# Cross-attention block: in half of the attention's units, scores are computed a second time with the keys on partitions instead of being turned, and the values' bias is added to the attention's result

## The chip, the cores and the metric

The kernel runs on one core of a Trainium2 chip. The metric is the time of one execution on the device, in microseconds (us), as the median of several runs. One execution was also recorded by the hardware profiler; where the text speaks of the profile or of the trace, it is that one.

## What is computed

The reference is one transformer block with cross-attention, in float32. Of B = 8 batches here, each has 256 tokens `x` and 256 context tokens, of width 512, with 16 heads of 32 elements.

```python
x = layer_norm(hidden_states, ln1_w, ln1_b)
q = (x @ q_w + q_b)   # split into 16 heads of 32
k = (encoder_hidden_states @ k_w + k_b)
v = (encoder_hidden_states @ v_w + v_b)
scores = einsum('bhqd,bhkd->bhqk', q, k) * scale
scores = where(mask, scores, mask_value)
out = einsum('bhqk,bhkd->bhqd', softmax(scores, axis=-1), v)
hidden = out @ cproj_w + cproj_b + hidden_states
y = layer_norm(hidden, ln2_w, ln2_b)
y = gelu(y @ fc_w + fc_b, approximate=True)      # 512 -> 2048
return hidden + y @ proj_w + proj_b              # 2048 -> 512
```

## The kernel before

**Groups and stages.** The eight batches are worked in two groups `g` of four. For each group there are stages, called streams: `ctx` (load and turn the context), `x` (load, normalise and turn the tokens), `k`, `q`, `v` (projections), `core` (attention), `o` (output projection), `y` (second normalisation), `fc` and `pr` (the two layers of the MLP). `fw` and `pw` make sums of the MLP's weights and store them in DRAM once, for both groups to load. The matrix products are made by a fast scheme of seven block products instead of eight (`quad`), in the MLP twice nested (`grown`, `grown2`); its sums of blocks are what `sums`, `plus` and `minus` issue on VectorE (DVE) or GpSimd (POOL), with names such as `z1i` or `y0t`. The products of one `quad` go to PSUM banks X, Y and W, from which `take` (a copy, on ScalarE (ACT) or DVE) or `plus` (an addition, on DVE) moves each result to SBUF.

**Attention.** A unit is four heads `hg` of one batch `b`; a group has 16 units. `scores` loads `q`, `k` and `v` of the unit, makes the group of matmuls `s` (eight matmuls on 32 rows of the array each, four heads side by side, into four banks, queries on partitions), adds the mask and takes each row's maximum on DVE (line 841, eight operations), and exponentiates on ACT with the row's sum accumulated (line 847, eight operations). The inverse sums and the maxima are turned on DVE (line 854), stored in DRAM (`rd`) and the inverse sums loaded back as `R` with queries along the free axis. `attend`, two units later (`LOOK = 2`), brings keys onto partitions: 16 turns on TensorE (PE) by the identity (line 870, tile `ps_pt`), four copies to `pt` (`take`), then the group `av` (eight matmuls, 32 columns of the array each), and the multiplication by `R` into the tile `att`.

**Bias of the values.** In `values_of` every fresh result of a `quad` is added to `vb`, the bias broadcast over all partitions, on the way out of PSUM. Other biases that lie along partitions come as columns: the vectors are loaded as rows, turned by PE (line 576) and kept in `cols`.

**Order.** Nothing is placed by hand. Every operation is entered into an `Order` with the engines that may run it and an estimated cost on each (`dve(n)`, `act(n)`, `pool(n)`, and given numbers), and with the tiles that it reads and writes. `times` gives each operation a due time: operations on PE from the window of their stage in `WINDOWS`, the others from their users, with `LEADS` for loads. `run` then goes through a planned execution and picks, for each engine that is free, the ready operation that is due first, within limits (`AHEAD`, `BORROW`, and `SWITCH` for a change of the array's shape, and free tiles and banks). Banks are three of a kind W and five of a kind C, of which C may be lent to W. Where an operation has several engines, this decides which gets it; operations marked `lock` are not planned on DVE and POOL at once. The instructions are issued in that order, so each engine works through a fixed list and waits where an input is late. All loads and stores are issued by one queue, SyncE (SP).

Of the kernel before, what the change touches and what calls it, by code (L numbers as in the profile page):

```python
# [12 lines left out]
U8 = mybir.dt.uint8  # L13
# [4 lines left out]
P = 128  # L18
# [11 lines left out]
BORROW = 25.6  # L30
SWITCH = 0.0

AHEAD = {"PE": 1000.0, "DVE": 66.7, "ACT": 36.8, "POOL": 25.4, "SP": 26.9}
# [19 lines left out]
class Order:  # L53
# [83 lines left out]
    def run(self):  # L137
# [29 lines left out]
        for o in ops:  # L167
            o.waiting = len(o.deps)
            o.ready = 0.0
        def offer(o):  # L170
            for e, _ in o.alts:
                cands[e].append(o)
        for o in ops:
            if not o.waiting:
                offer(o)
# [42 lines left out]
        while left:  # L218
            best = None
            for e in engines:  # L220
                pick, when = None, None
                soonest = None
                free = max(at[e], lanes[n_dma % DMA_LANES]) if e == "SP" else at[e]
                for o in cands[e]:
                    t = max(free, o.ready)
                    if soonest is None or t < soonest:
                        soonest = t
                if soonest is None:
                    continue
                t = max(soonest, skip[e])  # L230
# [6 lines left out]
            for o in cands[e]:  # L237
                if max(at[e], o.ready) > t + 1e-9:
                    x = max(at[e], o.ready)
                    again = x if again is None else min(again, x)  # L240
                    continue
# [87 lines left out]
            for x, _ in o.alts:  # L329
                cands[x].remove(o)  # L330
# [39 lines left out]
def pool(n):  # L370
# [11 lines left out]
    "ctx0": (2.1, 3.1, 6.2),  # L382
    "e0": (6.3, 7.3, 8.3),
    "e1": (2.7, 9.7, 23.1),
    "k0": (2.2, 19.8, 66.5),
    "x0": (41.0, 42.0, 52.6),
    "q0": (36.1, 69.2, 76.3),
    "v0": (51.8, 77.6, 120.0),
    "core0": (68.9, 154.0, 221.0),
    "ctx1": (81.1, 83.7, 113.7),  # L390
    "k1": (110.4, 118.8, 159.6),
    "v1": (152.1, 164.2, 181.7),
    "x1": (165.9, 169.4, 170.4),
    "q1": (191.8, 204.0, 224.7),
    "fw0": (42.7, 70.6, 89.3),
    "fw1": (104.3, 111.0, 140.7),
    "pw0": (140.8, 166.0, 168.9),
    "pw1": (181.8, 200.1, 227.1),
    "core1": (211.4, 327.0, 411.1),
    "o0": (225.3, 240.2, 271.2),  # L400
    "y0": (278.0, 297.0, 300.0),
    "fc0": (276.1, 365.9, 419.5),
    "o1": (427.1, 428.1, 463.4),
    "y1": (433.2, 448.9, 450.7),
    "pr0": (422.3, 480.5, 534.1),
    "fc1": (488.4, 556.6, 620.7),
# [849 lines left out]
```

## Time and profile before

| what | value |
|---|---|
| time, median of 3 runs | 720.68 us (718.65 to 720.99) |
| profiled execution, time | 720.62 us |
| profiled execution, span from first to last instruction | 718.6 us |
| granted TensorE clock, mean | 0.997 |
| PE busy, matmuls | 699.8 us, 4753 instructions |
| PE busy, weight loads (PEld) | 563.0 us |
| DVE busy | 592.1 us, 1382 instructions |
| ACT busy | 294.5 us, 829 instructions |
| POOL busy | 281.3 us, 261 instructions |
| DMA, share of 16 engines' time | 62.7%, 143.19 MB |

Busy time is the time in which an engine had at least one instruction under way. A float32 matmul appears as two instructions on PE. Matmuls overlap: the duration of one is longer than the distance to the next. On DVE and ACT, too, the next instruction starts some 0.1 us before the last one has ended, so the text uses distances from start to start where work is added up. Lines of the trace name a tile or tensor by what the program called it, without numbers; a tile's memory is reused, so a name in the trace may be that of an earlier tenant.

### The profile page before, as it was taken

The page shows a single profiled execution, that of the slowest core. Times are in us where ns is not written, and L with a number is a line of the kernel's source. Part 1 is how long each engine was busy: PE and PEld are TensorE (multiplying, and loading weights), DVE is VectorE, ACT ScalarE, POOL GpSimd, SP SyncE. Part 2 cuts the span into 40 slices and gives each one's busy share as a digit, 9 for nine tenths or more (in the row PEclk, how much of TensorE's full clock was granted, in tenths as well). Part 3 has the DMA queues.
Part 4 walks back from the last instruction along what each step waited for, and adds up shares of the span by engine and source line. Part 5 has one row for each costly group of instructions (what it writes and reads, how often), then busy time and mean ns, then how long its engine had stood idle before and what let it go on. Part 6 is the DMA issues. An engine that isn't in the chain of part 4 may idle for free.

```text
span 718.6 us, 13665 instructions
## 1 busy us (share of the span) xinstructions
PE 699.8 (97%) x4753; PEld 563.0 (78%) x4753; DVE 592.1 (82%) x1382; ACT 294.5 (41%) x829; POOL 281.3 (39%) x261
## 2 busy tenths in 40 slices
PE   6999999998999999999999999999999999998997
PEld 5555675566755687877788799999989988897997
DVE  2889589987898889888988867996579898997992
ACT  2243278657576656745659840120000107610000
POOL 1383046581563700030104588364677004843000
PEclk9999999999999999999999999999999999999999
DMA  7968875998789855274534743468666557730741
GB/s 232 327 205 313 306 252 183 283 337 283 206 281 317 278 183 169 78 219 146 161 94 143 256 123 100 148 204 245 183 180 182 160 157 246 278 103 1 247 150 59
DMA packets 119332, 144.06 MB, mean 200 GB/s; under 512 B 14136, under 2 KB 82272, under 8 KB 119264
## 3 DMA queue, kind: packets, MB, share of 16 engines
q1 hardware_dynamic: 119264, 143.19, 62.7%
q8 instruction: 38, 0.62, 0.4%
q14 instruction: 30, 0.25, 0.1%
HBM read 98.59 MB, written 44.56 MB: 199 GB/s over the span
## 4 chain that ended last, share of the span: by engine, by line
PE 90%; DVE 6%; DMA 2%; issue 1%; SPq 0%; POOL 0%; DVEq 0%; POOLq 0%
PE fc_X L541 13%; PE pr_X L541 13%; PE ps_pt L870 7%; PE fc_W L541 7%; PE pr_W L541 7%; PE s L541 5%; PE av L541 4%; PE k_X L541 4%; PE o_X L541 4%; PE q_X L541 4%; PE v_X L541 3%; PE fc_Y L541 3%; PE pr_Y L541 3%; PE o_W L541 2%; PE q_W L541 2%; PE v_W L541 2%
## 5 line engine op out<-in xcount | busy, mean ns | idle before, releaser
L847 ACT ACTIVATE pr<-pr,st 128x256 f32<-128x256 f32 x256 | 127.4, 502 | 82.3 <-DVE st L841 80.8
L841 DVE CUSTOM_DVE_ANT_0 pr<-s,mb 128x256 f32<-128x256 f32 x256 | 92.4, 418 | 10.1 <-PE s L541 9.9
L1030 ACT ACTIVATE h<-h,cols 128x256 f32<-128x256 f32 x128 | 54.3, 499 | 55.7 <-DVE h L532 52.7
L870 PEld LDWEIGHTS ps_pt<-ident,pr 128*128 128x128 f32 x512 | 59.4, 141 | 18.5 <-issue 5.6
L870 PE MATMUL ps_pt<-ident,pr 128*128 128x128 f32 x512 | 70.1, 275 | 2.4 <-DVE st L841 1.9
L532 DVE TENSOR_TENSOR h<-fc_X,h 128x512 f32<-128x512 f32 x80 | 54.3, 685 | 8.3 <-PE fc_X L541 8.1
L512 ACT COPY pt<-ps_pt 128x512 f32<-128x512 f32 x88 | 49.1, 579 | 24.6 <-PE ps_pt L870 20.5
L847 ACT ACTIVATION_READ_ACCUMULATOR pr<-pr,st 128x1 f32 x256 | 48.9, 191 | 0.0
L532 DVE TENSOR_TENSOR h<-fc_W,h 128x512 f32<-128x512 f32 x48 | 32.9, 686 | 5.3 <-PE fc_W L541 3.7
L541 PE MATMUL s<-ku,qu 32*128 32x256 f32 x512 | 36.9, 400 | 0.0
L541 PE MATMUL av<-pt,vu 128*32 128x256 f32 x512 | 35.0, 385 | 0.0
L541 PEld LDWEIGHTS s<-ku,qu 32*128 32x128 f32 x512 | 23.4, 184 | 13.5 <-issue 12.0
L512 ACT COPY e<-pr_X 128x256 f32<-128x256 f32 x4 | 1.5, 373 | 76.7 <-PE pr_X L541 76.7
L532 POOL TENSOR_TENSOR h<-h,fl 128x512 f32<-128x512 f32 x8 | 11.1, 1396 | 55.5 <-DVE fl L532 54.9
L541 PEld LDWEIGHTS av<-pt,vu 128*32 128x32 f32 x512 | 14.3, 109 | 20.1 <-issue 6.6
L532 DVE TENSOR_TENSOR po<-pr_X,po 128x256 f32<-128x256 f32 x40 | 16.7, 417 | 14.3 <-PE pr_X L541 14.3
L512 DVE COPY pt<-ps_pt 128x512 f32<-128x512 f32 x40 | 26.8, 683 | 1.8 <-PE ps_pt L870 1.1
L841 DVE DVE_READ_ACCUMULATOR2_ANT st<- 128x1 f32 x256 | 21.0, 82 | 0.0
L649 POOL TENSOR_TENSOR rs_y<-rs_y,neg_half 128x2 f32<-128x2 f32 x8 | 6.7, 836 | 35.8 <-DVE rs_y L646 35.7
L530 POOL TENSOR_TENSOR z0t<-h,h 128x512 f32<-128x512 f32 x12 | 15.0, 1272 | 13.3 <-PE fc_X L541 11.6
L530 POOL TENSOR_TENSOR z0i<-z0t,z0t 128x512 f32<-128x512 f32 x10 | 16.4, 1660 | 6.3 <-DVE y1t L532 3.3
L532 DVE TENSOR_TENSOR att<-av,r 128x256 f32<-128x256 f32 x32 | 13.4, 418 | 6.5 <-PE av L541 3.9
(643 smaller groups left out, 1841.7 us busy)
## 6 DMA issues: line engine op xcount, KB each, us to landing
fl<-prd SPq DMA_DIRECT2D x21, 256.0 KB
fl<-fcd SPq DMA_DIRECT2D x19, 256.0 KB
fw<-in_L_xattn_fc_w_dram SPq DMA_DIRECT2D x16, 256.0 KB
ku<-kd SPq DMA_DIRECT2D x32, 128.0 KB
vu<-vd SPq DMA_DIRECT2D x32, 128.0 KB
qu<-qd SPq DMA_DIRECT2D x32, 128.0 KB
r<-rd SPq DMA_DIRECT2D x32, 128.0 KB
pw<-in_L_xattn_proj_w_dram SPq DMA_DIRECT2D x32, 128.0 KB
```

The lines of the kernel that those rows point to most:

```text
L512: (nc.scalar.copy if e == "ACT" else nc.vector.tensor_copy)(to(), of_())
L530: nc.gpsimd.tensor_tensor(to()[:, ts(k, 512)], in0()[:, ts(k, 512)], in1()[:, ts(k, 512)], op)
L532: E[e].tensor_tensor(to(), in0(), in1(), op)
L541: nc.tensor.matmul(o(), l(), r(), start=first, stop=True, skip_group_check=True)
L649: lambda e, rs=rs: nc.gpsimd.tensor_tensor(tile_of(rs)[:, 2:4], tile_of(rs)[:, 0:2], neg_half[:, 0:2], ALU.pow), lock=True)
L841: nc.vector.tensor_tensor_reduce(at(p_, pk), at(sb[j], i), tile_of(mb), scale=-SCALE, scalar=FLT_MAX, op0=ALU.add, op1=ALU.min, accum_out= ...
L847: nc.scalar.activation(at(p_, pk), at(p_, pk), AF.Exp, bias=tile_of(st)[:, 8 + c : 9 + c], scale=-1.0, accum_out=tile_of(st)[:, 16 + c : 1 ...
L870: nc.tensor.transpose(at(ps, 2 * kc + i, 1, P), at(pr[j // 2], 2 * (j % 2) + i)[:, ts(kc, P)], ident.t)
L1030: lambda e, f=f, b=b, c=c: nc.scalar.activation(at(h[f][b], c), at(h[f][b], c), AF.Gelu_apprx_tanh, bias=col(c_fcb + f * 4 + c), scale=1.0 ...
```

## The change

In the units of `TWICE` (16 of the 32, eight in each group) the 16 turns and four copies are left out. Instead the maxima, which `rd` holds beside the inverse sums, are loaded as a second tile `M`, broadcast over all partitions (512 KB each). `attend` makes the scores again with `k` and `q` exchanged (group `t`, eight matmuls on 32 rows, into four banks, keys on partitions), subtracts the maxima on DVE (`sub`, four operations of 512 elements) and exponentiates in place on ACT (four operations of 512 elements), with the mask as a column for each half of the keys (`mcols`, made from rows of the mask that are turned with the other vectors). The first pass of scores, with its sums, stays as it is. The other 16 units turn as before.

The values' bias is no longer added in `values_of`; `vb` is a column, and a new operation adds it to `att` after the multiplication by `R`, on POOL, ACT or DVE. Further edits: the first half of group 0's context is turned tile by tile into four banks (`fine`); six `quad`s of `fc0` (`APART`) and the two of `o0` copy their fresh results out of PSUM and add in a second operation; the planner's constants `BORROW`, `SWITCH`, `AHEAD`, `WINDOWS` and `LEADS` have other values (the windows are not shown), and its bookkeeping of candidates is written anew.

```diff
-BORROW = 25.6
-SWITCH = 0.0
-AHEAD = {"PE": 1000.0, "DVE": 66.7, "ACT": 36.8, "POOL": 25.4, "SP": 26.9}
+BORROW = 30.3
+SWITCH = 0.82
+AHEAD = {"PE": 1000.0, "DVE": 70.9, "ACT": 33.0, "POOL": 25.4, "SP": 23.5}
...
+TWICE = {(g, hg, b) for g in range(2) for hg in range(4) for b in range(4) if (hg // 2 + b // 2) % 2 == 0}
+APART = {(f"fc{g}", p, s) for g in range(1) for p in (6, 5, 3) for s in range(2)}
...
-    vecs = [(ln1_w, 4), (ln1_b, 4), (q_b, 4), (k_b, 4), (ln2_w, 4), (ln2_b, 4), (fc_b, NF)]
+    vecs = [(ln1_w, 4), (ln1_b, 4), (q_b, 4), (k_b, 4), (ln2_w, 4), (ln2_b, 4), (fc_b, NF), (v_b, 4)]
     n_rows = sum(n for _, n in vecs)
-    rows = fixed("rows", [n_rows, P], keys=len(vecs))
+    n_cols = 64 + 2 * B
+    rows = fixed("rows", [n_cols, P], keys=len(vecs) + 1)
+    mrows = fixed("mrows", [n_cols, P], U8)
     cols = fixed("cols", [P, n_rows])
+    mcols = fixed("mcols", [P, 2 * B])
+    nc.gpsimd.memset(rows.t, 0.0)
...
+        load("mrows", mrows, None, lambda: mrows.t[64:, :], lambda: mask.rearrange("b (k p) -> (b k) p", p=P), 0.01)
+        T.op("mrows", [("DVE", 0.22)], [(mrows, None)], [(rows, [len(vecs)])],
+             lambda e: nc.vector.tensor_scalar_add(rows.t[64:, :], mrows.t[64:, :], -1.0))
...
+        T.op("mcols", [("DVE", 0.12)], [(ps, None)], [(mcols, None)],
+             lambda e: nc.vector.tensor_scalar(mcols.t, tile_of(ps)[:, 64:n_cols], FLT_MAX, SCALE, ALU.mult, ALU.mult))
+        for b, v in ((cb, cproj_b), (pb, proj_b)):
...
-    def turned(g, tag, tiles, copy):
+    def turned(g, tag, tiles, copy, fine=False):
         R = [[Buf(f"{tag}{g}_{J}{L}", "Q", 4) for L in range(2)] for J in range(2)]
         for L in range(2):
+            if fine and L == 0:
+                ps = [Buf(f"ps_{tag}{g}_{a}{L}", "C", 4) for a in range(4)]
+                for i in range(4):
+                    def fn(e, i=i, ps=ps):
+                        for a in range(4):
+                            nc.tensor.transpose(tile_of(ps[a])[:, ts(i, P)], tiles[i][1]()[:, ts(a, P)], ident.t)
+                    T.op(f"turn_{tag}{g}_{i}{L}", [("PE", 0.44)], [(tiles[i][0], None), (ident, None)], [(p_, [i]) for p_ in ps], fn, mode="full")
+                for a in range(4):
+                    copy(f"{tag}{g}_{a}{L}", R[a // 2][L], a % 2, ps[a], a)
+                continue
...
-        dst, bufs, add = {}, {}, {}
+        dst, bufs = {}, {}
...
-            add[il] = ((vb, None), lambda I=I: vb.t[:, None, ts(I, 256)].to_broadcast([P, 2, 256]))
-        project_plain(f"v{g}_{tp}", tp, L, R, dst, add, early)
+        project_plain(f"v{g}_{tp}", tp, L, R, dst, None, early)
...
+        M = None
+        if (g, hg, b) in TWICE:
+            M = Buf(f"m{u}", "Q", 4)
+            load(f"m{u}", M, None, lambda: tile_of(M),
+                 lambda: rd.t[8:16].rearrange("c a r -> (c a r)").partition_broadcast(P), 0.52, src=[(rd, None)])
...
-    def attend(g, hg, b, u, v, pr, R):
-        pt = [Buf(f"pt{u}_{h}", "Q", 2) for h in range(2)]
-        for j in range(4):
+        return u, q, k, v, pr, M, R
+    def attend(g, hg, b, u, q, k, v, pr, M, R):
+        pt = [Buf(f"pt{u}_{h}", "Q", 4) for h in range(2)]
+        if M is not None:
+            tb = [Buf(f"t{u}_{n}", "C", 2) for n in range(4)]
+            mm(f"t{u}", 0.97, [(q, None), (k, None)], [(t, None) for t in tb], [
+                (lambda j=j, kc=kc: at(tb[j], kc), lambda j=j, kc=kc: tile_of(k)[j * HD : (j + 1) * HD, ts(kc, P)],
+                 lambda j=j: tile_of(q)[j * HD : (j + 1) * HD, :], True)
+                for kc in range(2) for j in range(4)], mode="row")
+            two = lambda t: t.rearrange("p (k n) -> p k n", k=2)
+            for h in range(2):
+                for j in (2 * h, 2 * h + 1):
+                    T.op(f"sub{u}_{j}", [("DVE", dve(512))], [(tb[j], None), (M, [j])], [(pt[h], [2 * (j % 2), 2 * (j % 2) + 1])],
+                         lambda e, j=j, h=h: nc.vector.scalar_tensor_tensor(
+                             two(at(pt[h], j % 2, 1, 512)), two(tile_of(tb[j])), SCALE,
+                             at(M, j)[:, None, :].to_broadcast([P, 2, 256]), ALU.mult, ALU.add))
+                for kc in range(2):
+                    def exp2(e, h=h, kc=kc, c=2 * (4 * g + b) + kc):
+                        v = tile_of(pt[h]).rearrange("p (j k n) -> p j k n", j=2, k=2)[:, :, kc, :]
+                        nc.scalar.activation(v, v, AF.Exp, bias=mcols.t[:, c : c + 1])
+                    T.op(f"exp{u}t_{h}{kc}", [("ACT", 0.484)], [(pt[h], [kc, 2 + kc]), (mcols, None)], [(pt[h], [kc, 2 + kc])], exp2, table="exp")
+        for j in range(4 if M is None else 0):
...
+        def vbias(e):
+            if e == "ACT":
+                nc.scalar.activation(at(A, key), at(A, key), AF.Identity, bias=col(c_vb + hg), scale=1.0)
+            else:
+                E[e].tensor_scalar_add(at(A, key), at(A, key), col(c_vb + hg))
+        T.op(f"vb{u}", [("POOL", 0.75), ("ACT", 0.34), ("DVE", 0.22)], [(A, [key]), (cols, None)], [(A, [key])], vbias, lock=True)
...
-                if p in fused:
+                if p in fused and (name, p, s) in APART:
+                    dst, add = fused[p]
+                    quad(f"{name}{s}{p}", product_of(p), cost, dst)
+                    for k in IL:
+                        plus(f"{name}{s}{p}g_{k}", dst[k][0], dst[k][0], add[k][0], dst[k][1], dst[k][1], add[k][1], 512, pool_too=True)
+                elif p in fused:
...
-            project_plain(f"o{g}_{tp}", tp, W["o"], A, dst, dst)
+            if g == 0:
+                made = {il: Buf(f"om{g}_{tp}_{il}", "P") for il in IL}
+                two = {il: (lambda b=b: tile_of(b).rearrange("p (i n) -> p i n", i=2)) for il, b in made.items()}
+                project_plain(f"o{g}_{tp}", tp, W["o"], A, {il: ((b, None), two[il]) for il, b in made.items()}, None)
+                for il, b in made.items():
+                    plus(f"om{g}_{tp}_{il}", dst[il][0], dst[il][0], (b, None), dst[il][1], dst[il][1], two[il], 512, pool_too=True)
+            else:
+                project_plain(f"o{g}_{tp}", tp, W["o"], A, dst, dst)
```

## Prediction

> **What bounds the kernel now.** I read the page first (busy times, chain), then busy time by stage, then the order of time on PE, DVE and ACT inside the second attention. Page: span, busy time, and the chain that ended last.
> ```profile
> span 718.6 us, 13665 instructions
> ...
> PE 699.8 (97%) x4753; PEld 563.0 (78%) x4753; DVE 592.1 (82%) x1382; ACT 294.5 (41%) x829; POOL 281.3 (39%) x261
> ...
> PE 90%; DVE 6%; DMA 2%; issue 1%; SPq 0%; POOL 0%; DVEq 0%; POOLq 0%
> ```
> PE is 97% busy and carries 90% of the chain. The Trainium skill ("Trainium Kernel Development and Optimization", Performance Expectations) warns that matmul busy time is a bad measure, since matmuls overlap, and puts the weight loads' busy share above it; they are busy 78% here, so by that rule PE would have over a fifth to spare and taking work from it would bring nothing. I therefore price PE by start-to-start times, from the timeline of PE at 326 us:
> ```profile
> 326.85 1.03 PE L541 MATMUL fc_Y<-y,q 128*128 128x256 f32 x4
> 327.81 1.07 PE L541 MATMUL av<-pt,vu 128*32 128x256 f32 x16
> 328.81 1.15 PE L541 MATMUL s<-ku,qu 32*128 32x256 f32 x16
> 329.88 1.13 PE L541 MATMUL fc_W<-y0i,kws 128*128 128x256 f32 x4
> 330.85 1.03 PE L541 MATMUL fc_X<-y0i,ct 128*128 128x256 f32 x4
> 331.71 1.91 PE L870 MATMUL ps_pt<-ident,pr 128*128 128x128 f32 x16
> 333.46 1.03 PE L541 MATMUL fc_X<-y,xn_y 128*128 128x256 f32 x4
> 334.33 1.03 PE L541 MATMUL fc_X<-y,kws 128*128 128x256 f32 x4
> ```
> Columns: start, duration, instructions. Each start follows the one before with no idle time noted. Four full-size instructions 128x256 take 0.87 (333.46 to 334.33); 16 turns of scores 1.75 (331.71 to 333.46), so 0.109 each; a scores group `s`, 16 instructions on 32 rows, 1.07 (328.81 to 329.88); `av` 1.00. A full-size group before or after a 32-wide one takes 0.96 or 0.97: 0.09 for each change of shape. With these steps (128x512 and 128x128 products likewise: 0.43 and 0.112 an instruction) the before program's PE order adds up to 690.0 us of the 718.6. So PE sets the end; 28.6 us are lost, mostly in the first 8 us and after 612. By stage:
> ```profile
> core 0: us, PE busy (x) PEld busy (x) DVE busy (x) ACT busy (x) POOL busy (x), PEclk, DMA share, GB/s
> 85.00:235.00 150.00, 147.14 (x1055) 96.39 (x1054) 130.12 (x434) 101.05 (x323) 75.86 (x84) 1.00 0.83 269
> 235.00:394.00 159.00, 158.83 (x1162) 124.50 (x1161) 138.17 (x434) 105.14 (x317) 32.73 (x35) 1.00 0.54 161
> ...
> 612.00:719.00 107.00, 98.16 (x820) 96.14 (x818) 86.29 (x118) 13.68 (x34) 28.55 (x18) 0.98 0.41 136
> ```
> 85 to 235 is the first attention, 235 to 394 the second. In the second PE idles 0.2 us of 159 with DVE at 138.2 (87%): room, but not much.
>
> **PE.** In 16 of 32 units 16 turns go: 256 x 0.109 = 28.0 us removed. In each a group `t` of 8 matmuls (16 instructions of `s`'s shape) comes: 16 x 1.075 = 17.2. In the built orders (each engine's fixed list of instructions in the two programs) PE changes between full-size and 32-wide work 92 times before and 116 after: 24 x 0.09 = 2.2. Net -28.0 + 17.2 + 2.2 = -8.6 us; the after order adds up to 681.4. Everything else on PE keeps its count.
>
> **DVE.** The row for a PSUM-plus-SBUF operation of 512 elements:
> ```profile
> 332.73 0.69 DVE L532 TENSOR_TENSOR h<-fc_X,h 128x512 f32<-128x512 f32 x1
> 333.33 0.68 DVE L512 COPY pt<-ps_pt 128x512 f32<-128x512 f32 x1
> 333.93 0.68 DVE L532 TENSOR_TENSOR h<-fc_W,h 128x512 f32<-128x512 f32 x1
> 334.53 0.69 DVE L532 TENSOR_TENSOR h<-fc_X,h 128x512 f32<-128x512 f32 x1
> ```
> 0.60 start to start. `sub` is of that size and kind, but no row has its operation at 512; bounds are 0.60 and 0.72 (L619, the dearest 512-element operation from PSUM). I take 0.605, the same two sources. 64 x 0.605 = +38.7. Leaving: 5 copies, 30 adds of 512 from values, fc0 and o0, 23 weight sums of 256 (0.34) that the order puts on POOL, 3 of 1024 (1.14); arriving: 22 scalar additions of 256, 19 of them `vb` (0.3; bounds 0.20, L590, and 0.46, L662 at 512), and 5 adds of 256. All DVE work by start-to-start times: 535.5 before, 550.9 after. Between the `av` of unit 100 and that of 133 it goes from 133.2 against 158.4 of PE (84%) to 149.1 against 161.1 (93%). The profile's busy time there was 138.2, 1.04 times my sum; so 155 of 161 after: DVE still fits, with 4% left instead of 13%. In the first attention (units 000 to 033) it is 114.0 of 140.5 before, 115.7 of 134.4 after.
>
> **ACT.** The page has an in-place activation of 256 with a bias column (L1030) at 499 ns, five in 2.09 us: 0.42 each. Copies of 512:
> ```profile
> 332.42 1.06 ACT L512 COPY pt<-ps_pt 128x512 f32<-128x512 f32 x2
> 333.37 0.52 ACT L847 ACTIVATE pr<-pr,st 128x256 f32<-128x256 f32 x1
> ```
> 0.475 each, against 0.26 for 256: 0.21 per further 256 elements. So the new exp of 512 costs 0.42 + 0.21 = 0.63 (bounds 0.475 and 0.71, L660), where the planner counts 0.484. 64 x 0.63 = 40, less 11 copies, plus 12 `vb` and two table loads of 1.28: ACT goes from 284 to 327 us, far from binding as a sum.
>
> **The new path.** `av` of such a unit waits for four `sub` (2.42), the last two exps (1.26) and hand-overs of about 0.3: 4.0 us after `t` at best. With the dearer rows (4 x 0.72, 2 x 0.71) it is 4.6; add half to a whole operation queued ahead on DVE and ACT (0.3 to 1.1): 4.0 to 5.7. Between `t` and its `av` the built order holds 4.1 to 7.3 us of other PE work (five units have 4.7). Summing the shortfall over 16 units gives 0 at 4.0, 0.6 at 4.5, 3.3 at 5.0, 10.6 at 5.7. I take 3.0, a chain of 5.0, because the cheap rows are the near ones and each in-order queue adds some. Behind a late `av` on PE wait all later products; behind a late `sub` on DVE wait the evictions of fc0's banks.
>
> The Trainium skill ("TensorEngine Tiling (Array Packing)", Gotcha 1 and PSUM Bottleneck) speaks against the change: row tiles need a bank each, and emptying them becomes the limit. By that rule PE would stand 2.42 us for every `t`, 39 us in all, and the time would be near 750. The row at 329.88, where a full-size product follows `s` while DVE starts on its banks, shows no such wait.
>
> **DMA.** 16 loads of M, 512 KB each (8.4 MB on 143), stand on SP between the store of `rd` and the load of `r`: `r` is issued 0.55 later. From `s` to the issue of `rd` the trace has 8.5 us (328.81 to 337.33), 2.1 more to the next load, and the worst landing of `r` 7.24: 17.9 in all, 16.8 after `s` ends. The order has 13.7 (unit 033) and 14.1 (100) of PE work between `s` and `t` in the two tightest units, 16.7 or more in the others; the latter is 2 us slower at worst, so I count nothing beyond the 3.0. The planner moved other loads ahead, so the bytes issued between the `r` of unit 000 and of 100 per us of PE work are the same (44.8 MB in 149.7, 46.4 in 154.9).
>
> **The rest.** ctx0's turns run tile by tile: before, PE starts the last tile's turn at 7.63 and the first product at 10.46; nine of the thirteen turns in those 2.83 us move ahead of the last landing (2.0 us), but a copy (0.6) and its hand-over, hidden before, now follow the last turn: -0.9 (0 to -1.5). `vb`, 32 in all (19 DVE, 12 ACT, 1 POOL), lies between `av` and the sums of `o`, microseconds off PE's path: 0. fc0's and o0's split adds free their PSUM bank no later than the fused add did: 0, with 32 additions more on SBUF, partly POOL's, whose idle time hides them. POOL takes 26 half-tiles of pr1's sums instead of 16, pr1's products start earlier between fc1's; the 9 us lost after 612 may shrink by 5 or grow by 3: 0. The mask columns and the value column add an 80-row turn: 0.
>
> Sum on the profiled execution, 720.6 (span 718.6 and 2.0 around it; 0.1 from the median of 720.68): 720.6 - 8.6 - 0.9 + 3.0 = 714.1.
>
> **Rivals.** *A. The second pass ends after PE reaches `av`.* One mechanism: `sub` and exp queue behind fc0's evictions on DVE and the first exps on ACT. For it: DVE at 96% in the second attention, exp dearer than planned. Against: 0.2 us of PE idle there now. It needs 0.6 us of extra wait per unit to eat the 9.5 gained, 0.73 to be slower by 0.3%; at 1.2, 16 x 1.2 = 19: 730. *B. The gain goes to DMA in the first attention.* Between 144 and 180 the DMA share is 0.94 and PE loses 2.3 us of 36; if that held over 134 us, 8.6 us would go: 720.6 - 9.5 + 8.6 = 719.7. Against: the same bytes per us. *C. The reordered tail pays as well:* 5 of the 9 us after 612 return and the stalls stay at 0.7: 706.8. *D. It doesn't do what it says:* the orders show 256 turns and 128 new matmuls, so this is out.
>
> **Numbers.** Forecast 711 to 718.5: 0.55; C, 704 to 711: 0.15; B and weak forms of A, 718.5 to 722.8: 0.13; A, above: 0.17. A measurement of this kernel can tell about 0.3% (2.2 us). Faster 0.70, same 0.13, slower 0.17. Range: 720.6 - 8.6 - 1.5 + 0 - 5 = 705.5 below, 720.6 - 8.6 + 10.6 + 3 = 725.6 above; 705 to 725 leaves out about 0.2.
>
> **What would show it.** Right: PE rows of `ps_pt` 256, `t` at 1.07 a group, PE idle in the second attention below 5 us, DVE near 96% there. Wrong: `av` or a product waiting on ACT or DVE for over 10 us in all; `sub` above 0.72 or exp above 0.71; a landing of M that DVE waits for; `t` groups longer than `s`.

## The result and the profile after

The changed kernel takes 728.25 us (median of 4 runs, 724.73 to 729.13), the kernel before beside it 719.66 (718.14 to 720.99): a ratio of 1.0111, interval 1.0076 to 1.0146. Run again with other kernels it gave 1.0071 (1.0047 to 1.0094). It is slower by about 0.9%, 6.5 us, where 714.1 was forecast; 728 lies above the range as well. The profiled execution took 724.73 us. One execution among all the runs below, of e11, took 1837 us and is left out of every figure.

The page of the kernel after: span, busy time, the granted clock in 40 slices, the chain that ended last, and the groups of the second pass's exponent and subtraction.

```profile
span 722.9 us, 13903 instructions
...
PE 698.6 (97%) x4753; PEld 547.5 (76%) x4753; DVE 611.8 (85%) x1415; ACT 336.9 (47%) x895; POOL 331.2 (46%) x295
...
PEclk9999999989999999999999999999999999999999
...
PE 77%; DVE 11%; ACT 4%; DMA 4%; issue 2%; SPq 1%; POOL 0%; DVEq 0%; ACTq 0%; POOLq 0%
...
L910 ACT ACTIVATE pt<-pt,mcols 128x512 f32<-128x512 f32 x64 | 41.9, 714 | 13.8 <-DVE pt L904 9.8
...
L904 DVE SCALAR_TENSOR_TENSOR pt<-t,m 128x512 f32<-128x512 f32 x64 | 39.7, 679 | 0.6 <-PE t L546 0.6
```

PE's busy share still reads 97% and its busy time hardly moved, but PE's share of the chain fell from 90% to 77%; VectorE, ScalarE and DMA took what it lost. So PE now waits in more places. By stage, in the columns of the same view before:

```profile
core 0: us, PE busy (x) PEld busy (x) DVE busy (x) ACT busy (x) POOL busy (x), PEclk, DMA share, GB/s
85.00:235.00 150.00, 145.16 (x1025) 89.47 (x1026) 127.62 (x411) 104.29 (x308) 85.55 (x97) 0.98 0.88 285
235.00:402.00 167.00, 162.60 (x1177) 120.38 (x1174) 152.74 (x472) 122.50 (x349) 65.60 (x58) 0.99 0.60 183
612.00:722.00 110.00, 105.03 (x859) 101.50 (x858) 89.37 (x126) 16.02 (x38) 41.85 (x27) 1.00 0.42 135
```

In the first attention (85 to 235) the DMA share rose from 0.83 to 0.88 and PE idles 4.8 us instead of 2.9; in the second, 4.4 of 167 us instead of 0.2 of 159, at 91% VectorE; and both stages now have a clock below 1.

To see what was lost where, I add up PE's work in its fixed order by the prediction's steps, and take that sum from the start of a landmark in the profile; what is left is time in which PE waited or ran below full clock. (Up to the start of the last matmul the kernel before has 24.9 us of it; the prediction's 28.6 counts to the span's end.) Priced work: 689.8 us before, 681.1 after. Lost time, by stretch, us:

| up to | before | after | M a quarter (e2) | values' bias alone (e7) | second attention only (e8) |
|---|---|---|---|---|---|
| first scores | 9.2 | 7.7 | 8.8 | 12.1 | 11.8 |
| `av` of unit 001 | 4.0 | 6.2 | 1.8 | 2.1 | 3.3 |
| `av` of unit 100 | 0.2 | 3.8 | 2.1 | 0.5 | 1.1 |
| `av` of unit 110 | 1.4 | 7.6 | 7.3 | 1.5 | 8.8 |
| `av` of unit 133 | 0.4 | 3.8 | 3.9 | 1.6 | 2.5 |
| first product of `fc1` | 1.5 | 5.5 | 7.2 | 2.9 | 0.8 |
| end | 8.2 | 3.3 | 3.2 | 4.0 | 6.7 |
| sum | 24.9 | 37.9 | 34.3 | 24.7 | 35.0 |

The saving of 8.6 us of work is there. 13.0 us of lost time came on top (16.5 in a second profile of the same kernel, which has 41.4). The places are the middle of the first attention, its end, the start of the second, and the hand-over from the second attention to the output projection and the MLP's first product. What PE waited for between 100 and 260 us (target and releaser: us in total, times, longest):

```profile
PE ps_pt L918 <- DVE att L537: 2.1, 1, 2.1
PE q_W L546 <- DVE ows L537: 2.0, 1, 2.0
PE ps_pt L918 <- DVE st L865: 0.7, 1, 0.7
PE av L546 <- ACT pt L910: 0.3, 1, 0.3
```

The second pass's `av` waited 0.3 us in all; the turns of units without a second pass and a projection of the next group waited. VectorE, which released them, had itself waited for loads in the same stretch, of tokens `x` and of the output projection's weights:

```profile
DVE st_x L666 <- DMA xt<-in_x_dram: 4.2, 1, 4.2
...
DVE xt L537 <- DMA ct<-in_L_xattn_cproj_w_dram: 2.6, 1, 2.6
...
DVE ows L537 <- DMA qws<-in_L_xattn_cproj_w_dram: 1.5, 1, 1.5
```

The chain of the stretch 134 to 154 shows the first of these, in order of time:

```profile
138.71 0.43 SPq L504
139.14 0.04 issue
139.18 3.85 DMA xt<-in_x_dram
143.03 0.21 DVE pw0s L537
143.24 0.89 issue
144.13 0.19 DVE st L875
144.33 0.56 DVE st_x L666
144.89 0.32 DVE att L537
```

A load of x takes 3.85 us to land; VectorE's statistics of it (`st_x`) stand in its queue ahead of `att` and of a unit's maxima, and PE's turns of that unit's probabilities wait for these. In the six microseconds from 141 the DMA share is 1.05 (a transfer counts where it starts, so a full stretch can read above 1). Then the clock (columns as above; the last two rows cover the low part alone):

```profile
141.00:147.00 6.00, 3.16 (x13) 1.35 (x10) 5.30 (x15) 0.56 (x3) 2.49 (x2) 0.89 1.05 375
147.00:153.00 6.00, 6.00 (x18) 4.03 (x18) 4.26 (x18) 5.02 (x18) 2.49 (x4) 0.54 1.00 334
...
274.00:280.00 6.00, 3.85 (x39) 1.88 (x36) 5.97 (x15) 1.91 (x6) 5.55 (x3) 1.00 0.95 308
280.00:286.00 6.00, 5.52 (x27) 3.97 (x28) 5.32 (x23) 5.87 (x14) 4.83 (x5) 0.72 0.74 212
...
145.66:152.47 6.81, 6.12 (x19) 3.97 (x18) 5.44 (x22) 5.40 (x19) 3.14 (x4) 0.50 1.00 344
...
282.20:285.59 3.39, 3.39 (x20) 2.65 (x13) 3.12 (x9) 3.26 (x9) 2.39 (x3) 0.50 0.65 174
```

After each of the two long stalls PE ran at half clock, for 6.8 and for 3.4 us: 3.4 and 1.7 us more, beside the waits.

The largest single stall, before `av` of 110, is one `t` group:

```profile
276.21 1.15 PE L546 MATMUL s<-ku,qu 32*128 32x256 f32 x16
277.18 0.67 PE L546 MATMUL t<-qu,ku 32*128 32x256 f32 x2
280.48 3.15 PE L546 MATMUL t<-qu,ku 32*128 32x256 f32 x14 [2.63 <-DVE st L865]
283.57 0.47 PE L631 MATMUL ps_y<-ident,ows 128*128 128x128 f32 x1
```

It takes 6.39 us from its start to the next instruction, where each of the other 15 takes 1.07 or 1.08. It is the only one that comes right behind a group `s`; at least one group of full-size products or an `av` stands before every other. `t` and `s` need four banks each, and this `t` goes on only as VectorE takes the maxima of that `s` out of them.

### The profile page after: what moved, and what is told of

Read it like the earlier page. It is cut to its first block, busy times and chain, and to the rows that moved or that the text cites. A ratio compares the mean times of both kernels' runs of the same rounds, so it can differ in the third digit from the quotient of the medians.

```text
span 722.9 us, 13903 instructions
## 1 busy us (share of the span) xinstructions
PE 698.6 (97%) x4753; PEld 547.5 (76%) x4753; DVE 611.8 (85%) x1415; ACT 336.9 (47%) x895; POOL 331.2 (46%) x295
## 4 chain that ended last, share of the span: by engine, by line
PE 77%; DVE 11%; ACT 4%; DMA 4%; issue 2%; SPq 1%; POOL 0%; DVEq 0%; ACTq 0%; POOLq 0%
PE pr_X L546 12%; PE fc_X L546 11%; PE pr_W L546 6%; PE fc_W L546 5%; PE s L546 4%; PE v_X L546 3%; PE k_X L546 3%; PE ps_pt L918 3%; PE av L546 3%; PE q_X L546 3%; PE pr_Y L546 3%; PE o_X L546 3%; PE fc_Y L546 3%; PE t L546 2%; PE k_W L546 2%
## 5 line engine op out<-in xcount | busy, mean ns | idle before, releaser
L910 ACT ACTIVATE pt<-pt,mcols 128x512 f32<-128x512 f32 x64 | 41.9, 714 | 13.8 <-DVE pt L904 9.8
L537 DVE TENSOR_TENSOR h<-fc_X,h 128x512 f32<-128x512 f32 x56 | 38.1, 685 | 8.1 <-PE fc_X L546 7.9
L904 DVE SCALAR_TENSOR_TENSOR pt<-t,m 128x512 f32<-128x512 f32 x64 | 39.7, 679 | 0.6 <-PE t L546 0.6
L918 PE MATMUL ps_pt<-ident,pr 128*128 128x128 f32 x256 | 36.0, 282 | 3.1 <-DVE att L537 2.1
L918 PEld LDWEIGHTS ps_pt<-ident,pr 128*128 128x128 f32 x256 | 30.4, 144 | 10.8 <-DVE att L537 3.0
L517 ACT COPY h<-fc_X 128x512 f32<-128x512 f32 x29 | 16.8, 578 | 46.5 <-PE fc_X L546 45.1
L517 ACT COPY pt<-ps_pt 128x512 f32<-128x512 f32 x41 | 22.6, 580 | 9.4 <-PE ps_pt L918 9.3
L1228 POOL TENSOR_TENSOR hid<-hid,cb 128x1024 f32<-128x1024 f32 x7 | 17.4, 2505 | 20.6 <-DMA cb<-in_L_xattn_cproj_b_dram 17.8
L546 PE MATMUL t<-qu,ku 32*128 32x256 f32 x256 | 21.0, 407 | 2.6 <-DVE st L865 2.6
L546 PEld LDWEIGHTS t<-qu,ku 32*128 32x128 f32 x256 | 12.7, 185 | 11.3 <-DVE st L865 6.4
```

The costliest lines, as they stand in the source:

```text
L517: (nc.scalar.copy if e == "ACT" else nc.vector.tensor_copy)(to(), of_())
L537: E[e].tensor_tensor(to(), in0(), in1(), op)
L546: nc.tensor.matmul(o(), l(), r(), start=first, stop=True, skip_group_check=True)
L904: lambda e, j=j, h=h: nc.vector.scalar_tensor_tensor(two(at(pt[h], j % 2, 1, 512)), two(tile_of(tb[j])), SCALE, at(M, j)[:, None, :].to_br ...
L910: nc.scalar.activation(v, v, AF.Exp, bias=mcols.t[:, c : c + 1])
L918: nc.tensor.transpose(at(ps, 2 * kc + i, 1, P), at(pr[j // 2], 2 * (j % 2) + i)[:, ts(kc, P)], ident.t)
```

## Experiments

Three readings of the 13 us were stated at first. Theory 1: VectorE's 64 subtractions fill its queue, so that everything behind them comes late. Rival 2: the 8.4 MB of M fill the DMA queues, and landings come late. Rival 3: it is the rest of the change, the other constants of the order and the split additions. The runs were made at different times, each beside the kernel before, and are compared by their ratios to it; the kernel after stands at 1.007 to 1.011 on that scale, its middle at 1.009. A difference of 3 us or less is near the limit of what the intervals can tell. A "short" operation keeps its place in the order, so that every engine has the same list of instructions as the kernel after.

**e1, subtraction short, in the order of after.**

```diff
-  two(at(pt[h], j % 2, 1, 512)), two(tile_of(tb[j])), SCALE,
-  at(M, j)[:, None, :].to_broadcast([P, 2, 256]), ...
+  two(at(pt[h], j % 2, 1, 512))[:, :, :16], two(tile_of(tb[j]))[:, :, :16], SCALE,
+  at(M, j)[:, None, :16].to_broadcast([P, 2, 16]), ...
-  nc.scalar.activation(v, v, AF.Exp, ...)
+  nc.scalar.activation(v, still.rearrange("p (j n) -> p j n", j=2), AF.Exp, ...)
```

> The changed kernel in its own order, with each sub of the 64 working on 32 of its 512 columns (and the second exp reading a constant tile of the same size), so DVE is 64 x 0.53 = 34 us lighter and the second pass's chain 2.1 us shorter; the output leaves the second pass's subtraction out. Theory 1 (DVE is late because of the subs, and PE waits for DVE): most of the 13 us of extra PE stalls go, time 714 to 718 against 728. Rival 2 (late landings and M's DMA traffic): within 2 us of 728, since DVE waits for data and not for itself. Rival 3 (the new plan with its splits and reused buffers): at most 3 us gained.

723.94 us, ratio 1.0044 (1.0024 to 1.0065). VectorE's busy time fell by 29 us, the time by some 3 us. Theory 1 explains about half of the excess over before at most. PE's long waits between 100 and 300 us are as long as in the kernel after (the lines of kernel.py stand two further down):

```profile
PE ps_pt L920 <- DVE att L537: 2.7, 1, 2.7
PE t L546 <- DVE st L867: 2.6, 1, 2.6
PE q_W L546 <- DVE ows L537: 2.6, 1, 2.6
```

So the subtractions are not what the turns, `q_W` and `t` wait for. By the sums of the table above the stretch up to `av` of 133 shrinks, from 3.8 to about 1.5 us, and no other by more than 1 us.

**e2, M a quarter, in the order of after.**

```diff
-  load(f"m{u}", M, None, lambda: tile_of(M), lambda: rd.t[8:16]...partition_broadcast(P), ...)
+  load(f"m{u}", M, None, lambda: at(M, 0), lambda: rd.t[8:10]...partition_broadcast(P), ...)
-  two(tile_of(tb[j])), SCALE, at(M, j)...
+  two(tile_of(tb[j])), 0.0, at(M, 0)...
```

> The changed kernel in its own order, with M loaded for one head instead of four (128 KB instead of 512 KB, 6.3 MB less in all); the output uses the first head's maxima for all four. Theory 1 (DVE): no change, 727 to 729. Rival 2 (DMA): the stalls of the first attention after unit 010 (6.3 us) and before unit 100 (3.6 us) shrink, 721 to 725. Rival 3 (plan): no change.

720.4 us, ratio 0.9993 (0.9975 to 1.0011): 7 us less than after for 6.3 MB less. PE's waits between 100 and 260 us in it:

```profile
PE ps_pt L918 <- DVE st L865: 0.7, 1, 0.7
PE q_W L546 <- DVE ows L537: 0.3, 1, 0.3
PE av L546 <- ACT pt L910: 0.3, 1, 0.3
```

The two stalls of 2.1 and 2.0 us are gone or down to 0.3, in the same order of instructions; the table above has 6.1 us less in those two stretches, which puts them at 3.9, where the kernel before has 4.2. No other stretch gained more than 0.3 us. VectorE's waits for the loads named above shrank or went:

```profile
DVE xt L537 <- DMA ct<-in_L_xattn_cproj_w_dram: 2.4, 1, 2.4
DVE st_x L666 <- DMA xt<-in_x_dram: 2.2, 1, 2.2
```

This is not the luck of one execution: in the six profiles that run in this order up to 260 us with M whole (after, e13, e1, e5, e9, e18) the first of the two waits is 2.1 to 4.4 us, and the two stretches lose 10 to 12 us; in the two with M a quarter (e2 and e6 below) the wait is nil and the stretches lose 3.4 to 3.9. M's traffic is the largest single cause, and it acts in the first attention.

**e3, no second pass, everything else of the change.**

```diff
-  TWICE = {(g, hg, b) ... if (hg // 2 + b // 2) % 2 == 0}
+  TWICE = {(g, hg, b) ... if False}
```

> The changed kernel with no unit in TWICE, planned anew: all units turn, the rest of the change (constants, values' bias on the result, splits in fc0 and o0, tile-by-tile turns) stays. PE's work is 8.4 us more than with the second pass. Theory 1 (DVE is late because of the subs) and rival 2 (M's DMA): the extra stalls go, 718 to 722, as before. Rival 3 (the rest of the change and its plan make the stalls): the stalls stay and the work comes on top, 730 to 738.

734.6 us, ratio 1.0185 (1.0165 to 1.0206), as rival 3 had it. With the constants and splits that come with the change, but without the second pass, the kernel is slower still: 690.5 us of PE work and 39.0 lost. It looks as if the constants suited one list of operations and not another; no run shows that by itself.

**e4, the second pass in the order's old constants, without the splits.**

```diff
-  BORROW = 30.3 ; SWITCH = 0.82 ; AHEAD, LEADS and WINDOWS of the kernel after
+  BORROW = 25.6 ; SWITCH = 0.0  ; AHEAD, LEADS and WINDOWS of the kernel before
-  APART = {... for g in range(1) ...}   # and the split of o0, and ctx0's turns tile by tile
+  APART = {... for g in range(0) ...}
```

> The second pass and the values' bias on the result, but with the planner's constants, windows and leads of the kernel before, without the splits of fc0 and o0 and the tile-by-tile turns; planned anew. PE's work is 8.6 us less than before. Theory 1 (subs on DVE) and rival 2 (M's DMA): stalls as in the changed kernel or more, 726 to 735. Rival 3 (the new plan and the splits): 712 to 718.

730.08 us, ratio 1.012 (1.0092 to 1.0149), 43.7 us lost. The second pass costs as much without the splits and with the other constants, so rival 3 alone is not it (without the second pass the same order's constants give 0.9994, e7 below).

**e5, split additions short, and e6, with M a quarter too, both in the order of after.**

```diff
-  plus(..., dst[k][1], dst[k][1], add[k][1], 512, pool_too=True)
+  few = [lambda f=f: f()[:, :16] for f in (dst[k][1], dst[k][1], add[k][1])]
+  plus(..., *few, 512, pool_too=True)      # o0's eight additions likewise
```

> The kernel after, every engine in the same order, with the 32 separate additions that the split of the first output projection and of three first-group MLP products brings (8 and 24 of 128x512) made on 16 columns of 512; the rest of each sum is left out. Theory A (M's traffic costs some 8 us, and the rest of what the kernel after loses lies in GpSimd's additions, beside which two-element VectorE operations took 1.2 to 2.3 us instead of 0.15): the stall between av100 and av110 falls from 7.6 to about 2 us and the one before fc101 from 5.5 to about 2, so 717 to 722. Rival (the splits are free, as predicted, and these two stalls come from the order in which VectorE's queue was planned): 725 to 729, with the two stalls as they were.

724.9 us, ratio 1.0052 (1.0031 to 1.0072): some 3 us, less than theory A expected, and its two stalls stayed (7.2 before `av` of 110, 5.0 before `fc1`). As a cause of those two stalls the split additions are out. The stretch up to `av` of 133 falls here too, from 3.8 to about 1 us.

> The same with M loaded for one head in four as well (128 KB instead of 512 KB; the second pass takes the first head's maxima and a scale of zero, so its weights are not the attention's). Theory A: both losses go, and what the predicted TensorE saving of 8.6 us leaves is seen: 709 to 714. Rival (the splits are free): 719 to 722, as with the quarter M alone.

717.41 us, ratio 0.9946 (0.9917 to 0.9976). About 10 us below after, the sum of the two alone, and 7.6 us by the ratios below e5: M a second time. 30.2 us are lost; 9.1 of them lie in the stretch up to `av` of 110 and 5.0 in the one up to `fc1`, where the kernel before has 1.4 and 1.5. Those two stalls are what neither M nor the split additions explain.

**e7, the values' bias alone.** The diff of e4 with an empty `TWICE`.

> Nothing of the second pass, no splits, the constants of the order as in the kernel before; only the values' bias is added to the attention's result, and the order is planned anew. Theory A and the prediction: the bias costs nothing, 718 to 722. Rival (constants that suit one list of operations suit no other, and any change of the list costs some 10 us until they are chosen again): 726 to 734, with PE's lost time at 32 us or more instead of 24.9.

720.18 us, ratio 0.9994 (0.9973 to 1.0015), 24.7 us lost. The bias on the attention's result is free, as predicted, and a newly planned order with the old constants need not cost anything.

**e8, the second pass for 8 units of the second attention alone.** As e7 with

```diff
+  TWICE = {... if g == 1 and (hg // 2 + b // 2) % 2 == 0}
```

> As the run before, with the second pass for 8 units, all in the second attention, where the kernel before keeps its DMA engines busy 54% of the time instead of 83% in the first. By TensorE work alone 4.3 us below the run before it. Theory A (M is dear only where the DMA engines are near full): 3 to 5 us below the run before it. Rival (M or the longer VectorE queue costs as much here: VectorE was busy 87% of this stage): no faster than it, or up to 5 us slower.

726.96 us, ratio 1.0064 (1.0031 to 1.0096): 5 us (by the ratios) to 6.8 above e7 with 3.6 us less PE work. The expectation that the second attention has room was wrong; 8.8 us are lost at its start.

**e9, the residual's bias additions short, in the order of after.**

```diff
-  E[e].tensor_tensor(v(), v(), cb.t[:, None, :].to_broadcast([P, 2, D]), ALU.add)
+  E[e].tensor_tensor(v()[:, :, :8], v()[:, :, :8], cb.t[:, None, :8].to_broadcast([P, 2, 8]), ALU.add)
```

> The kernel after, every engine in the same order, with the 8 additions of the output projection's bias to the residual (128x1024, 2.35 us each on GpSimd) made on 16 of 1024 columns; the rest of that sum is left out. Theory C (between av100 and av110 these additions run on GpSimd beside VectorE's statistics, and VectorE's additions and two-element operations there take 2.1 and 1.2 us instead of 0.65 and 0.15, with the t group behind them): the stall of 7.6 us there falls to 3 to 4 and the time to 720 to 724. Rival D (t needs four PSUM banks that the maxima of the same unit's scores still hold, whatever GpSimd does): the stall stays at 6 to 8, 724 to 728.

722.28 us, ratio 1.0017 (0.9988 to 1.0045), some 5 us. The kernel after, VectorE and then GpSimd ahead of the stall at 277 (start, duration, instruction):

```profile
274.55 1.56 DVE L672 TENSOR_SCALAR rs_y<-mv_y 128x2 f32<-128x2 f32 x1
...
278.42 1.25 DVE L678 SCALAR_TENSOR_TENSOR rs_y<-mv_y,rs_y 128x2 f32<-128x2 f32 x1
```

```profile
273.71 2.36 POOL L1228 TENSOR_TENSOR hid<-hid,cb 128x1024 f32<-128x1024 f32 x1 [2.80 <-DMA hid<-in_x_dram]
...
277.31 2.34 POOL L1228 TENSOR_TENSOR hid<-hid,cb 128x1024 f32<-128x1024 f32 x1
```

The operations on two elements take 1.56 and 1.25 us and end at 276.11 and 279.67, when GpSimd's additions end (276.07 and 279.65). With these additions short, the same two:

```profile
275.90 0.17 DVE L672 TENSOR_SCALAR rs_y<-mv_y 128x2 f32<-128x2 f32 x1
...
279.48 0.13 DVE L678 SCALAR_TENSOR_TENSOR rs_y<-mv_y,rs_y 128x2 f32<-128x2 f32 x1
```

PE's `t` then waited 1.3 us instead of 2.6, and the group took 4.4 us instead of 6.4. So theory C's mechanism is shown, for about 2 us of this stall. The kernel before has as many of these long operations on two elements (five of 1.2 to 2.0 us; after: five of 1.2 to 2.3); what is new is that two of them stand ahead of `t`. The stall as a whole was 8.3 us in this profile, with the clock at 0.77 and 0.66 for the twelve microseconds from 280. What is left of it in `t` fits rival D: the banks that the maxima of the scores just before still hold. Where the rest of the 5 us was gained this profile does not show; it is one of the slower executions (725.02).

**e10, the first output projection not split.**

```diff
-  if g == 0:
+  if g < 0:
```

> The kernel after without the split of the first output projection alone (its quarters are added to the residual from PSUM, as in the kernel before); planned anew, in the same order up to about 225 us, where the residual's loads now stand 30 places earlier in SP's order. Theory C (the split let the residual's loads and with them GpSimd's bias additions fall into the stage of VectorE's statistics): the stall between av100 and av110 falls from 7.6 to 2 to 4 us, 720 to 724. Rival D (PSUM banks and VectorE's fuller queue): the stall stays, 725 to 730.

726.28 us, ratio 1.0059 (1.0029 to 1.0089), some 2 us less than after, which the intervals do not tell from nothing; the stall before `av` of 110 stayed (7.4). Moving the residual's loads forward did not cure it, and theory C is not the whole of that stall. What it is made of changed: eight turns of the second normalisation (`ps_y`) now stand between `s` and `t`, this `t` takes 2.84 us instead of 6.39, most of it at half clock, and PE waits 2.5 us at `ps_y` instead.

**e11 and e12, e8 with the subtraction short, and with M a quarter.** The diffs of e1 and e2, in e8's order.

> The kernel with the second pass in the second attention only, in its order, with the second pass's subtraction on VectorE on 32 of 512 columns and its exponent on a constant tile. If VectorE's 19 us of subtractions are what makes this kernel 6.8 us slower than the one with the values' bias alone: 719 to 722. If it is the PSUM banks of the t groups, or M: 724 to 728.

723.05 us, ratio 1.0024 (0.9997 to 1.0050): 3 us (by the ratios) to 3.9 less than e8, about half of the time that e8 costs over e7. 31.1 us are lost instead of 35.0; in the two stretches from `av` of 100 to `av` of 133 it is about 5 us less, of the 8 that e8 has there over e7.

> The kernel with the second pass in the second attention only, in its order, with M loaded for one head in four (128 KB instead of 512 KB; first head's maxima, scale zero). If M's traffic is dear in the second attention too: 720 to 723. If it is dear only where the DMA engines are near full: 725 to 727.

726.24 us, ratio 1.0090 (1.0060 to 1.0120): nothing gained. In the second attention, with a DMA share of 0.60, M is free; in the first, at 0.88, 7 us were to be had. That fits queues near full, though the two stages also differ in which loads stand beside M and in their order.

**e13, the kernel after once more.**

> The kernel after once more, unchanged, beside the kernels of this call. Each execution of it so far lay between 724.7 and 729.1 us; 725 to 729 again, 0.7% to 1.2% above the kernel before. If it lies lower, what the shortened kernels gained against it is smaller by as much.

727.01 us, ratio 1.0071; the level used above includes it.

**e14 and e15, four and eight units in the later half of the second attention.** As e7 with `TWICE` of `g == 1 and b % 2 == 1`, e14 with the parity of e8 as well.

> The kernel with the values' bias alone, and the second pass for 4 units, all in the later half of the second attention (b odd); in the same order as with the bias alone up to the second attention's start. Theory E (a unit's second pass is dear by its place: beside full DMA queues, or beside the first group's second layer norm at the start of the second attention, and free elsewhere): TensorE's saving of 2.2 us comes out, 716.5 to 720. Rival F (it is dear wherever it lies, by VectorE's 2.4 us a unit): 721 to 725.

721.99 us, ratio 1.0022 (0.9999 to 1.0044).

> The same with all 8 units of that half. Theory E: TensorE's saving of 4.3 us less one or two us for the VectorE queue, which has some 20 us of subtractions more in a stretch of 110 us: 716 to 720. Rival F: 724 to 729.

727.95 us, ratio 1.0086 (1.0059 to 1.0112). Theory E fell: late units are no cheaper. The five kernels with the old constants line up:

| units with a second pass | ratio | PE work, us | lost, us | lost per unit over e7 |
|---|---|---|---|---|
| 0 (e7) | 0.9994 | 689.8 | 24.7 | |
| 4, late (e14) | 1.0022 | 688.3 | 29.4 | 1.2 |
| 8, second attention (e8) | 1.0064 | 686.2 | 35.0 | 1.3 |
| 8, late (e15) | 1.0086 | 686.9 | 33.3 | 1.1 |
| 16 (e4) | 1.0120 | 681.3 | 43.7 | 1.2 |

**e16, e17, e18, one constant of the order moved,** in e7, e15 and the kernel after.

```diff
-  AHEAD = {..., "DVE": 66.7, ...}      # 70.9 in the kernel after
+  AHEAD = {..., "DVE": 68.7, ...}      # 68.9
```

> The kernel with the values' bias alone (720.2 us), the same operations, with one constant of the order moved: how far VectorE may run ahead, 68.7 instead of 66.7; the order differs from about 170 us on. Rival G (each order draws its own set of hand-offs that come late, so a kernel whose order was planned anew differs by several us whatever its operations are): 722 to 730. Rival F (the second pass is what costs, the order is not): 718.5 to 722.

717.88 us, ratio 0.9947 (0.9930 to 0.9965). This is a full version of the kernel, and it is faster than both.

> The kernel with eight late units (728.0 us) with the same constant moved in the same way. Rival G: anywhere from 718 to 728, more than 3 us from the 728.0 at even chance. Rival F: 725.5 to 730.

724.96 us, ratio 1.0052 (1.0032 to 1.0071).

> The kernel after with the same constant 2.0 lower (68.9 instead of 70.9); the order differs from about 430 us on alone. Rival G: the stall before fc101 and those behind it come out otherwise, 722 to 732 with more than 2 us between it and the kernel after. Rival F: 725 to 729.

727.78 us, ratio 1.0078 (1.0048 to 1.0108).

The constant moved the first two by 2.3 and 3.0 us, and left the kernel after where it was. Rival G is right that the order is worth up to some 3 us, but in both orders eight late second passes cost 7 to 8 us over none (728.0 against 720.2, 725.0 against 717.9). So with the old constants the cost goes with the second pass and not with one draw of the order. With the new constants and the rest of the change it is the other way round:

| ratio | without the second pass | with it, 16 units |
|---|---|---|
| old constants, no splits | 0.9994 (e7) | 1.0120 (e4) |
| new constants, splits | 1.0185 (e3) | 1.009 (after) |

It costs some 9 us in the first row and saves some 7 in the second. So a price of the second pass holds for the constants that it was measured with; what it would be with an order chosen for it alone, no run here tells. The profile of e16:

```profile
span 716.1 us, 13701 instructions
...
PE 698.1 (97%) x4753; PEld 560.8 (78%) x4753; DVE 592.3 (83%) x1402; ACT 301.8 (42%) x845; POOL 268.3 (37%) x251
...
PEclk9999999999999999999999999999999999999999
```

It does 8.7 us more PE work than the kernel after and ends 10 us earlier: 22.3 us lost, and its mean clock is 1.000.

## Why the prediction was wrong

What held. PE's work fell by the 8.6 us of the sum: the turns and the new groups cost what their rows said. The subtraction takes 0.60 us from start to start (679 ns for one; priced 0.605), the exponent 0.61 (714 ns; priced 0.63). The head gained 1.5 us (9.2 to 7.7), the far end of its bounds, in this profile; in the others with the same first instructions it stands at 8.0 to 8.9, nearer the 0.9 of the sum. The values' bias costs nothing (e7). The tail gave back 4.9 us (8.2 to 3.3), the full 5 of rival C, which the sum had at 0; e7, with the old constants, has 4.0 there too, so the reordering need not be what brings it. With these alone it would have been 720.6 - 8.6 - 1.5 - 4.9 = 705.6, near rival C's 706.8. Of the marks set for right, PE idles 4.4 us in the second attention, below the 5 named, but VectorE is busy for 91% there, not near 96%. Of those for wrong, PE's waits for VectorE and ScalarE come to 12.7 us over the span in the entries of 0.7 us or more (7.2 in the kernel before). 3.0 of them are turns; with the smaller entries `av` and products still have over the 10 named, though `av` has 0.3 of them.

What failed is the term for stalls, +3.0 us with 10.6 as its upper bound. The runs put 13.0 to 16.5 us more lost time on the profile even after head and tail had gained 6.4, so 19 us or more in between. By the table, 5.8 of them lie in the two stretches of the first attention, 6.2 before `av` of 110, 3.4 before `av` of 133 and 4.0 before the first product of `fc1`. Four steps of the working are behind it.

The first is "I count nothing" for M, and it accounts for the first attention. The argument was that bytes issued per microsecond stay the same; in the profile the DMA share of the first attention rose from 0.83 to 0.88, and with a quarter of M in the same order its two stretches lose no more than before (e2, e6). It had asked when M itself lands; VectorE never waited for M. Late were the loads queued with it, of x and of the output projection's weights, and in VectorE's fixed order the results that PE waited for stood behind them. Rival B had the right mechanism, with a chance of 0.13 shared with others.

The second is that `t` itself was taken to start without a wait: the row looked at had a full-size product behind `s`. For 15 groups that was right. The one that comes right behind `s` lost 5.3 us and, with the half clock that follows, is most of the stall before `av` of 110. No kernel here moves this group alone; e9 and e10, which shorten it to 4.4 and 2.8 us, change other things too.

The third is that only one wait was priced, `av` behind its own chain. That one was right: 0.3 us. In the old constants the series of 4, 8 and 16 units has 1.1 to 1.3 us lost for each second pass, where the sum had 0.19 (3.0 / 16) and PE saves 0.54 (8.6 / 16); there that alone turns the sign. The prediction's 4% of room on VectorE was a mean over 161 us. How much of the price is VectorE's queue is shown in part: with the subtractions short some 3 us come back in the order of after (e1), 3 to 4 in that of e8 (e11). Rival A's place was wrong; that its 1.2 us for a unit and its 730 come near what was measured is luck.

The fourth is "POOL's idle time hides them", for the split additions: short, they brought some 3 us. Why, no run shows; e9 shows for other GpSimd additions that an operation of VectorE can stand still beside one, so idle time of GpSimd alone does not make an addition free. The loss before `fc1` is gone in the orders of e10 and e18, and neither is faster for it by more than some 2 us; its cause stays open.

The Trainium skill ("TensorEngine Tiling (Array Packing)", Gotcha 1 and PSUM Bottleneck) says of row tiles that the copy out of PSUM may become the bottleneck. The prediction's estimate from that, 2.42 us at each of 16 groups, would have put the time near 750. The trace has PE at `t` behind banks that VectorE had not emptied once, in the group of 6.39 us. As a warning it was right; as a price for every group it was not.

Still open: e8 loses 10 us over e7; the subtractions account for about 4 of them (e11), M for nothing that the ratio shows (e12). At full clock one of its eight `t` groups takes 2.3 us instead of 1.1 and the others 1.0 to 1.1, so the banks account for about 1 more. The rest may be the order drawn around them. In e3 a stall of the same place (11.4 us) came without any second pass, with 6.1 us of it at `ps_y`, so the place is tender in some orders whatever the units do.

## What to carry to other kernels

When an engine at 97% is relieved by giving work to engines at 80 to 90%, price the queue behind each added operation and not only its own chain: in the old constants a second pass, whose own `av` hardly waited, went with 1.2 us of lost PE time a unit against 0.54 saved. Look in the built order for the one place where an added group stands right behind another that needs the same banks. A large load is not free because its consumer can wait; ask which loads share the queue, and read the DMA share of that stage. Test such a suspicion by shortening one operation in an unchanged order, and hold a newly planned order against a second draw of it before a difference of 3 us is put down to the change. Where a change comes with new constants of the order, run all four combinations: here the sign of the second pass depends on them.

## What the runs showed of the hardware

Stalls of PE cost more than their length. Beside the stretches of the kernel after shown above (0.54 and 0.72 over six microseconds, 0.50 in the low part alone), e7, which has no wait of PE above 1.5 us after the head, has a clock of 1.00 in the same stretches:

```profile
274.00:280.00 6.00, 6.00 (x50) 4.82 (x43) 5.59 (x22) 3.99 (x16) 0.00 (x0) 1.00 0.79 226
280.00:286.00 6.00, 5.83 (x57) 3.84 (x56) 5.73 (x26) 4.54 (x13) 1.09 (x2) 1.00 0.70 203
```

Over the whole span the mean clock is 0.993 after against 1.000 in e7, some 5 us of 722.9 (0.997 before, some 2). The Trainium skill ("TensorE: Matmul & The Clock Gate", What's actually happening) has the clock halved after an idle window of about 3.4 us. The half is what the trace shows (0.50); but here it fell after a single wait of 2.1 us (143.2 to 145.3), and in e11 after one of 1.8 us (0.72 in the six microseconds from 286), so shorter gaps were enough.

A VectorE operation on two elements, 0.13 to 0.17 us alone, took 1.25 and 1.56 us and ended with the GpSimd addition that ran when it began, while VectorE's maxima, which read a score from PSUM, stayed at 0.42 us with GpSimd beside them or not. The skill ("SBUF — State Buffer", SBUF: two separate sides) states that a port pair shared by the two is locked for a whole instruction, and these rows agree.
